# Layer 1's grouped product computed once in quarter-width tiles, with layer 0's full-array scores in place of its row-tiled transposed scores

## The chip, the core and the metric

The kernel runs on one NeuronCore of a Trainium2 chip. It has five engines that run side by side: TensorE (PE, matrix products; its weight loads are listed as PEld), VectorE (DVE), ScalarE (ACT), GpSimd (POOL) and SyncE (SP, which here only starts DMA transfers). Products land in PSUM, a small memory of eight banks of 128 partitions by 512 f32 values; DVE and ACT read it, POOL and DMA don't. SBUF is the working memory.

The metric is the device time of one execution in microseconds. Three runs of the kernel before took 5622.65, 5635.56 and 5646.51 us: the median is 5635.56.

## The reference

The input x is 2 images of 128 channels, 256 by 256, in f32. Two blocks follow each other, each a residual block: normalise (groups of 4 channels, over each image), apply the layer, add the input.

Layer 0 is windowed attention with a halo:

```python
qkv = einsum('bchw,oc->bohw', x, W_qkv)            # 128 -> 3*128, 4 heads of 32
q = 8x8 windows of q                               # 64 queries a window
k, v = 12x12 windows of k, v, step 8, padded by 2  # 144 keys a window
attn = (q * SCALE) @ k.T + rel_pos_emb(q) + FIXED_MASK
out = softmax(attn) @ v                            # back to the image
return einsum('bchw,oc->bohw', out, W_out)
```

The fixed mask is minus infinity except where row and column distance between query and key have the right parity. So the 64 queries of a window fall into four classes of 16 (row parity, column parity), and each class sees 36 of the 144 keys. The relative position term adds, for each query, one value by the column distance and one by the row distance.

Layer 1 is:

```python
t1 = conv(x, w1)                    # 5x1, 128 -> 128 channels
t3 = conv(t1, w3)                   # 3x1, each channel by itself
t2 = three copies of x, shifted by -2, 0, 2 columns
t4 = einsum('nckhw,ckg->nghw', t2, w4)   # 3*128 -> 8 channels
return t4[:, None] * t3.reshape(n, 16, 8, h, w)   # the 8 channels repeat 16 times
```

So t4 has 8 channels, and channel c of the output uses channel c mod 8 of t4.

## The kernel before

`kernel_body` runs three stages in a row: `attention_fast` (layer 0, lines 122 to 391), `in_range` (a test of the softmax denominators) and `convolutions_fast` (layer 1). After them a branch runs a second, complete implementation, `tile_halo_attention_then_conv`, if a denominator left its range; on the inputs at hand the branch isn't taken. Names of tiles in `attention_fast` begin with f_, and layer 1's tiles are xm, w, t, a, b, y, raw.

The image is worked in strips of 8 rows: 32 strips an image, 64 in all. In between, layer 0's output x1 lies in DRAM.

**Layer 0** begins with the statistics of image 0 (f_sx loads, line 88), about 92 us. Then it works units of one row parity of a strip: 128 units, two for each strip. The normalised strip is stored by row and column parity, so that all operands of a class lie together. A unit u does:

- `scores` (line 281): for each of 4 heads and 2 column parities ("lanes", 8) a 60 by 512 block of transposed scores, 60 keys of a pair of windows on partitions, 512 queries as columns. A lane uses 32 rows (one head's channels) and 60 columns of the array. It is filled by accumulation of 8 products for the column term (f_rw), 4 for the row term (f_rh) and 16 for the keys, one for each pair of windows (f_kt): 28 products in each of 8 lanes, 224 a unit.
- `numerators` (line 302): exponentials, with the mask as bias, no maximum subtracted.
- `values` (line 258): 32 products of 128 rows by 60 columns, copied from PSUM to f_vt by DVE (6 of 8 copies) and ACT (line 263).
- `attend` (line 317): 128 products of 60 rows by 32 columns, 33 moving columns (32 channels and the denominator), followed by reciprocal, scaling and a 32 by 32 block transpose on DVE (`head_outputs`).
- `project` (line 342), `queries` (line 245) and `keys` (line 232): products of the full array with 512 columns.

The order of PE's instructions in layer 0 is written out by hand (`manual_schedule`); the other engines' order, and layer 1's, is set by the scheduler.

**Layer 1** works strip by strip. For each strip k: normalise 8 rows (line 442, DVE; POOL copies 4 rows of overlap, line 440); t1 by four groups of five products, 128 by 128 weights and 512 columns, one for each tap of w1 (line 482), copied by ACT (486); t3 by one ACT scaling (488) and two DVE multiply-adds over 2048 values (490); then for each two rows t4 by three products (line 497), of which the weights w4 are tiled 16 times so that all 128 output channels come out, and y = t4 times t3 by DVE from PSUM (501); two additions of the input by POOL (505, 506) and a store from POOL's queue (507). So t4 costs 12 products of 512 columns a strip. PSUM: three banks for a, three for b.

Of the kernel before, what the change touches and what calls it, by code (L numbers as in the profile page):

```python
# [10 lines left out]
I32 = mybir.dt.int32  # L11
# [5 lines left out]
PE = mybir.EngineType.PE  # L17
# [9 lines left out]
XC = 130  # L27
XW = 272

DEN_LOW, DEN_HIGH = 1.0e-24, 1.0e36  # L30

# [9 lines left out]
def host_constants():  # L46
    ident = np.eye(P, dtype=np.float32)
    gavg = np.zeros((P, P), np.float32)
    for g in range(P // 4):
        gavg[4 * g : 4 * g + 4, 4 * g : 4 * g + 4] = 0.25  # L50

    kb = np.zeros((HEADS, 32, 6, 10), np.float32)
    for c in range(10):
        kb[:, c, :, c] = 1.0
    for r in range(6):
        kb[:, 10 + r, r, :] = 1.0
    kb[:, 16, :, 6:] = NEG
    kb[:, 17, :, :4] = NEG
    flag = np.zeros((2, 4 * NPAIR * 4, 2, 4), np.float32)
    flag[0, :, 0] = 1.0  # L60
    flag[1, :, 1] = 1.0

    mask = np.full((2, 64, 2), NEG, np.float32)
    for key in range(60):
        c = key // 6
        mask[:, key, 0] = 0.0 if c < 6 else NEG
        mask[:, key, 1] = 0.0 if c >= 4 else NEG
    return {
        "c_ident": ident,
        "c_gavg": gavg,  # L70
        "c_kb": kb.reshape(P, 60),
        "c_flag": flag.reshape(2, 4 * NPAIR, 32),
        "c_mask": mask.reshape(P, 2),
    }


class Norms:


    def __init__(self, nc, glob, small, gavg, ns):  # L80
        self.nc, self.glob, self.small, self.gavg, self.ns = nc, glob, small, gavg, ns

    def new(self, name, tag):
        return self.glob.tile([P, self.ns * 4, 6], F32, tag=tag, name=name)

    def chunk(self, st, n, t):
        for c in range(t.shape[1] // 2):
            self.nc.vector.bn_stats(  # L88
                st[:, n + c, :], t[:, 2 * c : 2 * c + 2, :].rearrange("p a w -> p (a w)")
            )  # L90

    def group(self, st, ps_pool, name):
        nc, glob, small, gavg = self.nc, self.glob, self.small, self.gavg
        mv = small.tile([P, 2], F32, tag="mv", name=f"mv_{name}")
        nc.vector.bn_aggr(mv, st.rearrange("p n k -> p (n k)"))  # L95
        pm = ps_pool.tile([P, 512], F32, tag="pj", name=f"pm_{name}")
        nc.tensor.matmul(pm[:, 0:1], gavg, mv[:, 0:1], start=True, stop=True)
        mean = glob.tile([P, 1], F32, tag=f"mean_{name}", name=f"mean_{name}")
        nc.vector.tensor_copy(mean, pm[:, 0:1])
        d = small.tile([P, 1], F32, tag="d", name=f"d_{name}")  # L100
        nc.vector.tensor_sub(d, mv[:, 0:1], mean)
        q = small.tile([P, 1], F32, tag="q", name=f"q_{name}")
        nc.vector.tensor_mul(q, d, d)
        nc.vector.tensor_add(q, q, mv[:, 1:2])
        pv = ps_pool.tile([P, 512], F32, tag="pj", name=f"pv_{name}")
        nc.tensor.matmul(pv[:, 0:1], gavg, q, start=True, stop=True)
        v = small.tile([P, 1], F32, tag="v", name=f"v_{name}")
        nc.vector.tensor_scalar(v, pv[:, 0:1], 1e-5, None, ALU.add)
        sd = small.tile([P, 1], F32, tag="sd", name=f"sd_{name}")
        nc.scalar.activation(sd, v, AF.Sqrt)  # L110

        r0 = small.tile([P, 1], F32, tag="r0", name=f"r0_{name}")
        nc.vector.reciprocal(r0, sd)
        nc.vector.tensor_mul(r0, r0, v)
        nc.vector.tensor_add(r0, r0, sd)
        nc.vector.tensor_scalar(r0, r0, 0.5, None, ALU.mult)
        rstd = glob.tile([P, 1], F32, tag=f"rstd_{name}", name=f"rstd_{name}")
        nc.vector.reciprocal(rstd, r0)
        return mean, rstd


def attention_fast(tc, io, x1_d, norm, st_x, st_y, tags, rc_all):

    nc = tc.nc
    x = io["x"]
    NB, _, H, _ = x.shape
    NS = H // 8
    NU = 2 * NB * NS
    with ExitStack() as l0:
        cst = l0.enter_context(tc.tile_pool(name="f_cst", bufs=1))  # L130
        ps_pj = l0.enter_context(tc.tile_pool(name="f_pj", bufs=2, space=PSUM))
        ps_s = l0.enter_context(tc.tile_pool(name="f_s", bufs=1, space=PSUM))
        ps_o = l0.enter_context(tc.tile_pool(name="f_o", bufs=1, space=PSUM))

        def cload(name, src, shape):
            t = cst.tile(shape, F32, tag=f"f_{name}", name=f"f_{name}")
            nc.sync.dma_start(t, src)
            return t

        wqkvT = cload("wqkvT", io["w_qkvT"], [P, 3 * P])  # L140
        woT = cload("woT", io["w_outT"], [P, P])
        mask = cload("mask", io["c_mask"], [P, 2])
        rw = cload("rw", io["rw"], [P, 8, 60])
        rh = cload("rh", io["rh"], [P, 4, 60])
        wq_s = cst.tile([P, P], F32, tag="f_wq_s", name="f_wq_s")
        nc.scalar.mul(wq_s, wqkvT[:, 0:P], SCALE)
        wkT = wqkvT[:, P : 2 * P]
        wvT = wqkvT[:, 2 * P : 3 * P]

        xn = [cst.tile([P, 2, 2, XC, 6], F32, tag=f"f_xn{i}", name=f"f_xn{i}") for i in range(2)]  # L150
        kt = [
            [cst.tile([P, 2, XC, 6], F32, tag=f"f_kt{r}{i}", name=f"f_kt{r}{i}") for i in range(2)]
            for r in range(2)
        ]
        vt = [
            cst.tile([P, NPAIR, HEADS, 33], F32, tag=f"f_vt{i}", name=f"f_vt{i}") for i in range(2)
        ]
        sc = [ps_s.tile([P, 512], F32, tag=f"s{h}", name=f"f_s{h}") for h in range(HEADS)]
        for i in range(2):
            nc.gpsimd.memset(xn[i], 0.0)  # L160
            for r in range(2):
                nc.gpsimd.memset(kt[r][i], 0.0)
            nc.gpsimd.memset(vt[i], 1.0)
        for h in range(HEADS):
            nc.vector.memset(sc[h], 0.0)

        with ExitStack() as setup:
            sp = setup.enter_context(tc.tile_pool(name="f_setup", bufs=6))
            for s in range(NS):
                t = sp.tile([P, 8, W], F32, tag="sx", name=f"f_sx_0_{s}")  # L170
                nc.sync.dma_start(t, x[0, :, 8 * s : 8 * s + 8, :])
                norm.chunk(st_x[0], 4 * s, t)

        rawp = l0.enter_context(tc.tile_pool(name="f_raw", bufs=4))
        x1p = l0.enter_context(tc.tile_pool(name="f_x1", bufs=2))
        wk = l0.enter_context(tc.tile_pool(name="f_wk", bufs=2))

        raws, norms, qs, pts, ots, x1s, po = {}, {}, {}, {}, {}, {}, {}

        def stats_chunk(b, c):  # L180

            t = rawp.tile([P, 4, W], F32, tag="sx", name=f"f_sx_{b}_{c}", bufs=2)
            nc.sync.dma_start(t, x[b, :, 4 * c : 4 * c + 4, :])
            norm.chunk(st_x[b], 2 * c, t)

        def load_rows(k):

            b, s = divmod(k, NS)
            t = rawp.tile([P, 10, W], F32, tag="raw", name=f"f_raw_{k}")
            n = min(10, H - 8 * s)  # L190
            nc.sync.dma_start(t[:, 0:n, :], x[b, :, 8 * s : 8 * s + n, :])
            raws[k] = t

        def normalise(k):
            b, s = divmod(k, NS)
            if s == 0:
                norms[b] = norm.group(st_x[b], ps_pj, f"x{b}")
                st_y[b] = norm.new(f"st_y{b}", tags[(2 * b + 2) % 3])
                if b + 1 < NB:
                    st_x[b + 1] = norm.new(f"st_x{b + 1}", tags[(2 * b + 1) % 3])  # L200
            mean, rstd = norms[b]
            cur, prev = xn[k % 2], xn[(k + 1) % 2]
            cells = cur.rearrange("p r c j i -> p (r c) j i")
            if s == 0:
                nc.gpsimd.memset(cells[:, :, :, 0:1], 0.0)
                lo = 0
            else:
                nc.gpsimd.tensor_copy(
                    cells[:, :, :, 0:2], prev.rearrange("p r c j i -> p (r c) j i")[:, :, :, 4:6]
                )  # L210
                lo = 1
            hi = min(10, H - 8 * s) // 2
            rows = raws[k].rearrange("p (i r) (j c) -> p c r j i", r=2, c=2)
            for c in range(2):
                nc.vector.tensor_scalar(
# [119 lines left out]
        def project(u, half):  # L335
# [14 lines left out]
            if half == 1:  # L350
                nc.gpsimd.dma_start(x1_d[b][s][:, r:8:2, :], x1)  # L351
                norm.chunk(st_y[b], 4 * s + 2 * r, x1)
                if r == 1:
                    del raws[k]
# [183 lines left out]
def in_range(tc, glob, rc_all):  # L538
# [19 lines left out]
    return good  # L558

# [555 lines left out]
```

## Time and profile before

| | us |
|---|---|
| median of three runs | 5635.56 |
| the profiled execution's own time | 5622.65 |
| its span, first to last instruction | 5620.7 |
| start: statistics of image 0 | 0 to 97.6 |
| layer 0 | 97.6 to 3829.3 |
| range test, statistics of layer 0's output | 3829.3 to 3844.7 |
| layer 1 | 3844.7 to 5620.7 |

| line, engine | what | count | mean ns |
|---|---|---|---|
| L486 ACT | a to t, 128 by 512 | 254 | 585 |
| L488 ACT | t3 scaling, 128 by 2048 | 64 | 2002 |
| L490 DVE | multiply-add, 128 by 2048 | 128 | 2530 |
| L442 DVE | normalise, 128 by 2048 | 62 | 1338 |
| L263 DVE | f_pv to f_vt, 60 by 512 | 768 | 687 |
| L332 DVE | transpose, 128 by 512 | 256 | 711 |

How the page is read: busy time is the time in which an engine worked on something, and the idle time behind a bar "|" is that of the engine just before an instruction of the group, with what ended it. "issue" is idle time that nothing in the profile explains. The granted clock is the share of TensorE's full clock. The chain goes back from the last instruction, at each step to what released it.

### The profile page before, as it was taken

To read this page: it belongs to the slowest core of one execution; us is meant where nothing else is said; L and a number is where in the kernel's file an instruction comes from. 1 tells how busy PE (TensorE), PEld (TensorE's weight loads), DVE (VectorE), ACT (ScalarE), POOL (GpSimd) and SP (SyncE) were. 2 spreads that over 40 slices of the span, in tenths; PEclk is the share of its full clock that TensorE was granted. 3 is DMA by queue.
4 is the path that set the end of the run, shared out by engine and by line. 5 is a ranking of instruction groups with operands and counts; after the bars stand their busy time and mean duration, and the time that the engine had idled before them with its cause. 6 is when DMAs were issued, how large, how long until landed. Compare 5 with 4: busy or idle time off the path is not lost.

```text
span 5620.7 us, 217714 instructions
## 1 busy us (share of the span) xinstructions
PE 4597.4 (82%) x103982; PEld 2896.5 (52%) x103982; DVE 2227.0 (40%) x3705; ACT 1131.0 (20%) x2133; POOL 844.7 (15%) x656
## 2 busy tenths in 40 slices
PE   2677777777777777777777777778999999999998
PEld 1555555555555555555555555554444444444443
DVE  8754334343433444334343433434333333333333
ACT  1122222222222222222222222221111111111111
POOL 1000000000000000000000000002322232333222
PEclk9778878787778788778878887888999999999999
DMA  8521111111111111111111111102222222222221
GB/s 323 196 79 50 37 41 50 41 50 41 48 43 35 50 41 50 41 37 50 41 50 41 50 41 37 48 22 79 79 79 75 75 75 75 75 81 76 82 75 50
DMA packets 71310, 367.08 MB, mean 65 GB/s; under 512 B 8080, under 2 KB 8848, under 8 KB 49936
## 3 DMA queue, kind: packets, MB, share of 16 engines
q1 hardware_dynamic: 42768, 218.82, 11.8%
q0 software_dynamic: 27648, 134.23, 5.9%
q8 instruction: 818, 13.40, 1.0%
q14 instruction: 76, 0.62, 0.0%
HBM read 218.80 MB, written 134.22 MB: 63 GB/s over the span
## 4 chain that ended last, share of the span: by engine, by line
PE 76%; issue 15%; DVE 6%; DMA 2%; ACT 1%; SPq 0%; POOL 0%; ACTq 0%; POOLq 0%; DVEq 0%
PE a L482 19%; PE f_s L281 17%; PE b L497 12%; PE f_pv L258 10%; PE f_o L317 6%; DVE f_vt L263 5%; PE f_pk L232 4%; PE f_pq L245 4%; PE f_py L342 3%; DMA f_sx<-in_x 2%; ACT f_vt L263 1%; DVE f_st_x L88 1%; DVE st_x L88 0%; PE a_first L468 0%; DVE mv_x L95 0%
## 5 line engine op out<-in xcount | busy, mean ns | idle before, releaser
L263 DVE COPY f_vt<-f_pv 60x512 f32<-60x512 f32 x768 | 527.4, 687 | 1751.4 <-PE f_pv L258 1742.5
L482 PE MATMUL a<-xm,w 128*128 128x512 f32 (+1 forms) x2560 | 1105.6, 589 | 0.0
L281 PE MATMUL f_s<-f_q,f_kt 32*60 32x32 f32 x32768 | 522.8, 264 | 375.7 <-issue 375.7
L258 PE MATMUL f_pv<-f_wqkvT,f_xn 128*60 128x128 f32 x8192 | 758.2, 356 | 71.3 <-DVE f_vt L263 56.0
L482 PEld LDWEIGHTS a<-xm,w 128*128 128x128 f32 x2560 | 480.9, 188 | 614.5 <-issue 613.3
L302 ACT ACTIVATE f_p<-f_s,f_mask 128x256 f32<-128x256 f32 x1024 | 388.0, 488 | 1795.8 <-PE f_s L281 1795.8
L258 PEld LDWEIGHTS f_pv<-f_wqkvT,f_xn 128*60 128x60 f32 x8192 | 665.1, 181 | 141.6 <-PE f_pv L258 82.1
L490 DVE SCALAR_TENSOR_TENSOR t<-t,w,t 128x2048 f32<-128x2048 f32 x128 | 323.8, 2530 | 1014.1 <-ACT t L486 1011.9
L281 PEld LDWEIGHTS f_s<-f_q,f_kt 32*60 32x60 f32 x32768 | 498.2, 175 | 409.0 <-issue 408.1
L497 PE MATMUL b<-xm,w 128*128 128x512 f32 x1536 | 669.5, 591 | 0.0
L351 POOL DMA_DIRECT2D f_x<-f_x x128 | 91.2, 713 | 2955.8 <-DVE f_x L345 2955.8
L281 PE MATMUL f_s<-f_q,f_rw 32*60 32x64 f32 x16384 | 258.1, 252 | 295.5 <-issue 295.5
L497 PEld LDWEIGHTS b<-xm,w 128*128 128x128 f32 x1536 | 289.5, 189 | 368.9 <-issue 367.2
L486 ACT COPY t<-a 128x512 f32<-128x512 f32 (+1 forms) x256 | 149.3, 583 | 1451.9 <-PE a L482 1451.9
L317 PEld LDWEIGHTS f_o<-f_vt,f_p 60*32 60x32 f32 x32768 | 303.2, 105 | 224.8 <-issue 125.2
L281 PEld LDWEIGHTS f_s<-f_q,f_rw 32*60 32x60 f32 x16384 | 219.7, 145 | 317.5 <-issue 312.2
L281 PE MATMUL f_s<-f_q,f_rh 32*60 32x128 f32 x8192 | 314.4, 406 | 71.2 <-issue 71.2
L317 PE MATMUL f_o<-f_vt,f_p 60*32 60x33 f32 x32768 | 334.4, 201 | 28.3 <-issue 26.6
L342 PE MATMUL f_py<-f_ot,f_woT 128*128 128x512 f32 x512 | 287.3, 649 | 45.0 <-ACT f_vt L263 32.6
L281 PEld LDWEIGHTS f_s<-f_q,f_rh 32*60 32x60 f32 x8192 | 231.9, 175 | 101.9 <-issue 100.5
L232 PE MATMUL f_pk<-f_xn,f_wqkvT 128*128 128x512 f32 (+1 forms) x528 | 266.5, 625 | 4.3 <-issue 3.0
L506 POOL TENSOR_TENSOR y<-y,raw 128x1280 f32<-128x1280 f32 x64 | 244.7, 3823 | 127.4 <-DVE y L501 127.4
(90 smaller groups left out, 3043.9 us busy)
## 6 DMA issues: line engine op xcount, KB each, us to landing
f_raw<-in_x SPq DMA_DIRECT2D x62, 1280.0 KB, 6.8
f_x<-f_x POOLq DMA_DIRECT2D x128, 512.0 KB, 5.2
out<-y POOLq DMA_DIRECT2D x64, 1024.0 KB, 4.2
raw<-f_x SPq DMA_DIRECT2D x64, 640.0 KB, 4.2
f_sx<-in_x SPq DMA_DIRECT2D x32, 1024.0 KB, 12.2
f_sx<-in_x SPq DMA_DIRECT2D x64, 512.0 KB, 3.6
raw<-f_x SPq DMA_DIRECT2D x62, 384.0 KB, 4.8
f_raw<-in_x SPq DMA_DIRECT2D x2, 1024.0 KB, 5.6
```

What stands on the lines that cost most here:

```text
L232: nc.tensor.matmul(pk[:, : n * P], wkT, xt[:, r, c, 1:129, lo:hi], start=True, stop=True)
L245: nc.tensor.matmul(pq, wq_s, xn[k % 2][:, r, c, 1:129, 1:5], start=True, stop=True)
L258: nc.tensor.matmul(pv[64 * c : 64 * c + 60, P * n : P * n + P], xt[:, r, c, col : col + 10].rearrange("p j i -> p (j i)"), wvT, start=True ...
L263: (nc.scalar.copy if c and j > 1 else nc.vector.tensor_copy)(vt[u % 2][64 * c : 64 * c + 60, 4 * j : 4 * j + 4, :, 0:32], pv[64 * c : 64 * ...
L281: nc.tensor.matmul(out, w, m, start=start, stop=stop, skip_group_check=True)
L302: nc.scalar.activation(p[:, h].rearrange("p (n e q) -> p n e q", e=2, q=16)[:, :, e], sc[h].rearrange("p (n e q) -> p n e q", e=2, q=16)[: ...
L317: nc.tensor.matmul(po[c][32 * h : 32 * h + 32, n, :], p[rows, h, 32 * m : 32 * m + 32], v[rows, m, h, :], start=True, stop=True,)
L342: nc.tensor.matmul(py, woT, ots.pop((u, half)), start=True, stop=True)
L482: nc.tensor.matmul(pa[:, : n * W], w1[:, tap, :], xt[:, j - 2 + tap : j - 2 + tap + n, 2 : 2 + W], start=tap == 0, stop=tap == 4,)
L490: nc.vector.scalar_tensor_tensor(t3, t1[:, tap : tap + 8, :], w3[:, tap : tap + 1], t3, ALU.mult, ALU.add)
L497: nc.tensor.matmul(pb, w4[:, tap, :], xt[:, j + 1 : j + 3, 2 * tap : 2 * tap + W], start=tap == 0, stop=tap == 2,)
L506: nc.gpsimd.tensor_tensor(y[:, 3:8, :], y[:, 3:8, :], raws[b, s][:, 0:5, :], ALU.add)
```

## The change

Two things change together.

Layer 0 is now the first half of `tile_halo_attention_then_conv`, which the program before held behind the branch; `attention_fast`, `in_range`, `convolutions_fast` and the branch go. Its work:

- A strip is worked in 8 units i: four classes ab (row and column parity), each in two halves of 8 pairs of windows. 512 units in all.
- `queries` (once a class): one product of 512 columns, copied by four ACT copies of 32 partitions into a block-diagonal tile qbd (two buffers).
- `unfold` (once a class): POOL copies the normalised strip to xu, 60 keys of each of 16 pairs of windows together.
- `biases` (once a strip): 32 products, 128 by 128 weights wb and 64 columns; 16 ACT copies of 16 partitions put the terms into abd (one buffer), 16 rows of bias terms and two mask flags for each head.
- `scores`: for each of 8 pairs of windows two products with 128 weight columns (4 heads by 32 queries) and 60 moving columns (keys): qbd with the keys, and abd with the constant kb. So scores lie with queries on partitions. DVE takes the maximum and subtracts it, ACT exponentiates.
- `transposes`: four 128 by 128 transposes on TensorE, copied by DVE or ACT in turn, before `attend`, which has the products of before.
- No order is written out by hand.

Layer 1 computes t4 once, for 8 channels padded to 32: four row pairs j go to four 32-partition blocks of one PSUM bank, 12 products with 32 weight columns. ACT copies the bank to t4; then for each j one product with a 0/1 matrix (32 rows, 128 columns) spreads the 8 channels to 128. In the program's order one product of the next strip's t1 stands ahead of these four. PSUM: two banks for a, one for g, four for b.

```diff
-        ps_a = l1.enter_context(tc.tile_pool(name="ps_a", bufs=3, space=PSUM))
-        ps_b = l1.enter_context(tc.tile_pool(name="ps_b", bufs=3, space=PSUM))
+        ps_a = l1.enter_context(tc.tile_pool(name="ps_a", bufs=2, space=PSUM))
+        ps_g = l1.enter_context(tc.tile_pool(name="ps_g", bufs=1, space=PSUM))
+        ps_b = l1.enter_context(tc.tile_pool(name="ps_b", bufs=1, space=PSUM))
...
-        w4 = cst.tile([P, 3, P], F32, tag="w4", name="w4")
+        w4 = cst.tile([P, 3, 32], F32, tag="w4", name="w4")
+        sel = cst.tile([P, P], F32, tag="sel", name="sel")
+        nc.sync.dma_start(sel, io["c_sel"])
...
+            pg = ps_g.tile([P, 512], F32, tag="g", name=f"g_{k}")
+            for tap in range(3):
+                for j in range(4):
+                    nc.tensor.matmul(
+                        pg[32 * j : 32 * j + 32, :], w4[:, tap, :],
+                        xt[:, 2 * j + 1 : 2 * j + 3, 2 * tap : 2 * tap + W],
+                        start=tap == 0, stop=tap == 2,
+                    )
+            t4 = wk.tile([P, 512], F32, tag="t4", name=f"t4_{k}")
+            nc.scalar.copy(t4, pg)
...
-            for j in range(0, 8, 2):
-                pb = ps_b.tile([P, 512], F32, tag="b", name=f"b_{k}_{j}")
-                for tap in range(3):
-                    nc.tensor.matmul(
-                        pb, w4[:, tap, :], xt[:, j + 1 : j + 3, 2 * tap : 2 * tap + W],
-                        start=tap == 0, stop=tap == 2,
-                    )
+            for j in range(4):
+                pb = ps_b.tile([P, 512], F32, tag=f"b{j}", name=f"b_{k}_{j}")
+                nc.tensor.matmul(
+                    pb, sel[32 * j : 32 * j + 32, :], t4[32 * j : 32 * j + 32, :], start=True, stop=True
+                )
...
-        kernel_body(tc, io, out)
+        tile_halo_attention_then_conv(tc, io, out)
```

The functions of layer 0 that take over, from the kernel after:

```python
def biases(k):
    xv = xn[k % 2].rearrange("p r (k c) -> p r c k", c=16)
    for t1 in range(4):
        pa = ps_pj.tile([P, 512], F32, tag="pj", name=f"pa_{k}_{t1}")
        for v in range(8):
            ...
            nc.tensor.matmul(
                pa[:, 64 * v : 64 * v + 64],
                wb[:, t1, v].rearrange("p h r -> p (h r)"),
                xv[:, 2 + 2 * t1 : 4 + 2 * t1, c : c + 2, k0 : k0 + NPAIR],
                start=True, stop=True,
            )
        for h in range(HEADS):
            nc.scalar.copy(
                abd[32 * h : 32 * h + 16, :, :, h, t1, :].rearrange("p k n v -> p (k n) v"),
                pa[32 * h : 32 * h + 16, :].rearrange("p (v m) -> p m v", v=8),
            )

def scores(i):
    k, g = divmod(i, 8)
    ab, half = divmod(g, 2)
    ps = ps_s.tile([P, 8, 64], F32, tag="s", name=f"s_{i}")
    for j in range(8):
        c0 = 8 * (8 * half + j)
        dst = ps[:, j, 0:60]
        nc.tensor.matmul(
            dst, qbd[ab % 2][:, 8 * half + j].rearrange("p h t v -> p (h t v)"),
            kt[k % 2][:, ab, :, c0 : c0 + 10], start=True, stop=False,
        )
        nc.tensor.matmul(
            dst, abd[:, ab, 8 * half + j].rearrange("p h t v -> p (h t v)"), kb,
            start=False, stop=True,
        )
    mx = wk.tile([P, 8, 1], F32, tag="mx", name=f"mx_{i}")
    nc.vector.tensor_reduce(mx, ps[:, :, 0:60], AX.X, ALU.max)
    p = pt[i % 3]
    nc.vector.tensor_tensor(p[:, :, 0:60], ps[:, :, 0:60], mx.to_broadcast([P, 8, 60]), ALU.subtract)
    nc.scalar.activation(p[:, :, 0:60], p[:, :, 0:60], AF.Exp)

def transposes(i):
    p = pt[i % 3]
    pp = ps_t.tile([P, 4, P], F32, tag="t", name=f"t_{i}")
    for j in range(4):
        nc.tensor.transpose(pp[:, j, :], p[:, 2 * j : 2 * j + 2, :].rearrange("p a b -> p (a b)"), ident)
    t = wk.tile([P, 4, P], F32, tag="ptT", name=f"ptT_{i}")
    if i % 2:
        nc.scalar.copy(t, pp)
    else:
        nc.vector.tensor_copy(t, pp)
    pts[i] = t
```

The other functions of layer 0 (`queries`, `keys`, `unfold`, `values`, `attend`, `head_outputs`, `project`) do per class or half what the description above says.

## The prediction

> **What bounds the kernel now.** I read the page's busy shares and slices first, then the busy time by stage, then the groups, then the order of time inside a stage.
>
> ```profile
> PE 4597.4 (82%) x103982; PEld 2896.5 (52%) x103982; DVE 2227.0 (40%) x3705; ACT 1131.0 (20%) x2133; POOL 844.7 (15%) x656
> ...
> PE   2677777777777777777777777778999999999998
> ...
> PEclk9778878787778788778878887888999999999999
> ...
> PE 76%; issue 15%; DVE 6%; DMA 2%; ACT 1%; SPq 0%; POOL 0%; ACTq 0%; POOLq 0%; DVEq 0%
> PE a L482 19%; PE f_s L281 17%; PE b L497 12%; PE f_pv L258 10%; PE f_o L317 6%; DVE f_vt L263 5%; PE f_pk L232 4%; PE f_pq L245 4%; PE f_py L342 3%; DMA f_sx<-in_x 2%; ACT f_vt L263 1%; DVE f_st_x L88 1%; DVE st_x L88 0%; PE a_first L468 0%; DVE mv_x L95 0%
> ```
>
> TensorE sets the time: 76% of the chain that ended last is its work, with 15% of "issue". The slices show two stages. Windows cut at their ends (us; busy time and count of PE, PEld, DVE, ACT, POOL; clock, DMA share, GB/s):
>
> ```profile
> 97.60:3829.30 3731.70, 2835.14 (x99860) 2119.90 (x99860) 1551.68 (x3085) 849.45 (x1805) 292.46 (x318) 0.80 0.16 52
> 3844.70:5620.70 1776.00, 1758.57 (x4108) 773.46 (x4108) 576.43 (x449) 278.02 (x322) 531.23 (x322) 0.99 0.20 74
> ```
>
> Layer 0 takes 3731.7 us, 58.3 us for each of 64 strips, at a mean clock of 0.80 with PE 76% busy. Layer 1 takes 1776.0, 27.75 a strip, PE 99% busy: what leaves PE there shortens the kernel, down to the next limit (DVE 9.0 us a strip, POOL 8.3).
>
> ```profile
> L482 PE MATMUL a<-xm,w 128*128 128x512 f32 x2540 | 1101.3, 590 | 0.0
> L482 PEld LDWEIGHTS a<-xm,w 128*128 128x128 f32 x2560 | 480.9, 188 | 614.5 <-issue 613.3 <-POOL y L505 0.5
> L281 PE MATMUL f_s<-f_q,f_kt 32*60 32x32 f32 x32768 | 522.8, 264 | 375.7 <-issue 375.7
> L235 ACT COPY f_kt<-f_pk 128x512 f32<-128x512 f32 x256 | 155.0, 606 | 95.6 <-PE f_pk L232 95.6
> L501 DVE TENSOR_TENSOR y<-b,t 128x512 f32<-128x512 f32 x256 | 170.7, 688 | 161.6 <-PE b L497 155.0 <-DVE t L490 1.1
> ```
>
> Line 482 issues 1280 products and the trace holds 2560 loads: an f32 product is two pairs of weight load and matmul. The timeline gives the price of a pair by its shape:
>
> ```profile
> 1923.16 0.30 PEld L97 LDWEIGHTS pm_x<-mv_x,f_gavg 128*128 128x128 f32 x2
> ...
> 3016.43 0.87 PEld L258 LDWEIGHTS f_pv<-f_wqkvT,f_xn 128*60 128x60 f32 x16 [0.76 <-PE f_pv L258]
> 3016.46 1.09 PE L258 MATMUL f_pv<-f_wqkvT,f_xn 128*60 128x128 f32 x16 [0.54 <-DVE f_vt L263]
> ...
> 3021.47 1.29 PE L317 MATMUL f_o<-f_vt,f_p 60*32 60x33 f32 x128
> 3022.69 1.99 PE L245 MATMUL f_pq<-f_xn,f_wq_s 128*128 128x512 f32 x4
> ...
> 4507.09 17.34 PE L482 MATMUL a<-xm,w 128*128 128x512 f32 x40
> ```
>
> - 512 columns: 0.43 us a pair (17.34/40), the load hidden behind the stream.
> - 128 weight columns, one moving column: two loads take 0.30 us and one 0.19, so the second costs 0.11. A product with few columns is bound by its load.
> - Values (L258), two column tiles side by side: 1.09 us for 16 pairs.
> - Heads (L317), eight tiles: (3022.69 - 3021.47)/128 = 0.0095 us a pair.
>
> **The change, part by part.** *Layer 0* gets full-array scores. Out, per strip: 448 row-tiled products (896 pairs). The chain puts f_s at 17% (956 us), and the waits put 742 us on "issue" in front of f_s: 26.5 us a strip together. Also out are the waits of the values for DVE's copies (f_vt, 5%, 4.4 us a strip): the new order has other groups between two value groups, and ACT takes half of the copies. In or kept, on PE per strip (8 units of 16 windows, in the order of the built program):
>
> - scores: 128 products, 256 pairs x 0.11 = 28.2 us (60 moving columns stream in 0.43 x 60/512 = 0.05, so the load binds);
> - position biases: 32 products, 64 pairs x 0.11 = 7.0;
> - transposes: 32. Every f32 product of the trace is two pairs: 64 x 0.11 = 7.0. Lower end one pair, 3.5;
> - kept work: values 8 x 1.09 = 8.7; heads 512 x 0.0095 = 4.9; queries, keys and projection 12 products, 24 x 0.43 = 10.3;
> - change of shape between groups, 24 a strip: f_pq starts 0.07 before the modelled end of f_o, so little is lost; 0.1 each, 2.4 (ends 0 and 6.7, the 0.28 by which f_pq's 1.99 exceeds 4 x 0.43).
>
> 68.5 us. Not shown before: queries and keys now stream every second column (before, runs of four), and the biases' columns lie 64 bytes apart. Bounds: nothing, or the stream of 8 products at half rate, 8 x 0.86 = 6.9 us; below nothing it can't go, since f_pq streams as fast as the contiguous L482. I take nothing, by f_pq; the biases are bound by their loads.
>
> Waits: `abd` has one buffer, so a new strip's bias copies follow the old strip's last scores. From there: first bias group 1.8, 16 ACT copies x 0.606 = 9.7, one exponential 0.6, four query copies 2.4 = 14.5 us before the next scores; PE has 11.3 to do (7.0 + heads 0.6 + transposes 0.9 + queries 0.9 + values 1.1 + projection 0.9): 3.2 idle. The three later query blocks each wait for four copies and an exponential (0.9 + 0.1 + 2.4 + 0.6 = 4.0 against 3.4 of PE work): 0.6 x 3 = 1.8. Behind the waiting scores stand the next values and heads. Sum 73.5 us a strip; ends 64 (transposes of one pair, no idle at the start, free changes of shape) and 80 (dear changes of shape, query waits doubled). DVE: per unit a maximum and a subtraction over 480 (0.65 each by L501's rate), copies, head outputs, about 4.4 us of 9.2; ACT 4.2; POOL's unfolding (960 elements four times a strip, 1.1 to 2.0 ns each by its strided copies L208 and L227) 4 to 8 of 73, on two buffers: all beside PE. SP's row loads shrink from ten rows to eight; the DMA engines were 16% busy. 64 x 73.5 = 4704, against 3731.7: **+972**.
>
> [...]
>
> [...]
>
> *Head and seam.* The range test goes (two reductions of 4.4 us at 3824 to 3834, -9); 64 small bias-weight copies on DVE come into the start (0.16 each by the one-column rows, +10), where DVE is busy with statistics. Nothing net; new POOL memsets lie beside the 92 us of loads.
>
> *Layer 1.* Out: 24 pairs x 0.43 = 10.3 us a strip. In: 24 pairs in four 32-column tiles, and 8 pairs in four 32-row tiles. Two column tiles ran fully side by side in f_pv (0.87/16 = 0.054 a pair against 0.43 x 128/512 = 0.107), eight tiles of f_o at least 2.9-fold (0.43 x 33/512 = 0.0277 against 0.0095). I take fourfold: 2.6 + 0.9, plus four changes of shape at 0.15: 4.1, saving 6.2. Twofold (5.2 + 1.7 + 0.6) saves 2.8; not at all (13.7 + 0.6) costs 4.0. The new wait (product, ACT copy 0.6, spread) is covered by the next strip's first product, 0.86, which stands ahead of the spread; if ACT were late, the other 19 products queue behind it. The normalisation of the next strip now stands behind the first tap: 0.6 + 2.0 + 2.5 + 1.3 after the sixth row, 6.8 with hand-overs against 4.3 + 2.6 on PE: just covered. The small weights' and the selector's loads lie ahead of the stage. 64 x 6.2 = **-397**.
>
> Sum: the profiled run's 5622.65 (span 5620.7 and 2 around it) + 972 - 397 = 6198. That run was the fastest of three, 13 below the median: **6210 us**.
>
> **Rivals.**
> 1. *Faster: the score loads overlap each other.* 320 pairs a strip; each 0.01 us is 205 us, so under 0.08 a pair the kernel is faster than before. At the streaming limit of 0.05 it takes 6210 - 1230 = 4980. For it: eight-tile loads overlap in L317. Against: L97's pairs stream a single column and still come 0.11 apart.
> 2. *Layer 0 loses less:* transposes of one pair (-224) and no idle at strip starts (-205): 5780. For: DVE and ACT under half busy; against: the single `abd`.
> 3. *The clock.* Before, layer 0 ran at 0.80 on the mean: after gaps on "issue" the clock fell to 0.5 for several us. The new stream has a third fewer instructions and shorter gaps, so I take full clock. At 0.80 its 68.5 us become 86: +1100, 7300.
> 4. *Layer 1's tiles do not run side by side:* +4.0 in place of -6.2 a strip, 6860; at twofold, 6430.
>
> **How the numbers follow.** My forecast (6000 to 6450) 0.50; rival 2 (5600 to 6000) 0.20, of which 0.03 within 0.5%; rival 3 0.10; rival 4 0.10; rival 1 0.10. About 0.5% (28 us) is what a measurement of this kernel can tell from no change. Faster 0.10, same 0.03, slower 0.87. The range, 5720 to 6900, leaves out rival 1 and the tail of rival 3; it holds rival 2's sum and rival 4's, and strided streams at half rate (6650).
>
> **What would show it.** Layer 0 near 4700 us with score loads 0.11 apart; t products twice or once per transpose; PE idle about 3 us before the first scores of a strip, ended by ACT; clock near 1; layer 1 near 1380 with four g matmuls starting within 0.1 us. Score pairs under 0.08, or a clock of 0.8, make it wrong.

## The result and the profile after

The kernel after takes 6175.03 us (median of four runs, 6154.85 to 6200.46) against 5641.03 for the kernel before (four runs): 1.0954 times as long, 95% interval 1.0902 to 1.1007. The forecast was 6210 us. The profiled execution took 6200.46 us; the prediction's sum for it was 6198 (the profiled execution of before plus the two terms). By the medians the change costs 534 us, where the forecast had 574 (6210 against 5635.56).

The same stages as before, cut at their ends (us; busy time and count of PE, PEld, DVE, ACT, POOL; granted clock, DMA share, GB/s):

```profile
103.80:4799.00 4695.20, 4524.11 (x65042) 3797.67 (x65042) 2113.41 (x4037) 2033.22 (x3597) 534.00 (x766) 0.94 0.11 37
4816.00:6198.70 1382.70, 1366.59 (x4617) 536.23 (x4616) 601.29 (x448) 315.50 (x386) 470.19 (x322) 0.99 0.26 96
```

Layer 0 went from 3731.7 to 4695.2 us (+963.5; forecast +972), layer 1 from 1776.0 to 1382.7 (-393.3; forecast -397). The start before layer 0 grew by 6.2 us and the seam between the layers by 1.6. The four add up to 578.0, the whole difference of the two spans.

On the page, PE is now almost always busy, and the clock is nearly full, where before it lay at 7 to 8 tenths throughout layer 0:

```profile
PE 5899.2 (95%) x69684; PEld 4339.8 (70%) x69684; DVE 2814.9 (45%) x4720; ACT 2353.2 (38%) x3993; POOL 1039.0 (17%) x1112
...
PE   3999999999999999999999999999999999999998
...
PEclk9999899998999999899999999999999999999999
```

The groups of instructions on PE (line, out<-in, shape, count; busy us, mean ns of one; idle before, and what ended it):

```profile
L322 PE MATMUL s<-kt,qbd 128*128 128x60 f32 x8192 | 1687.5, 289 | 12.4 <-ACT qbd L294 4.1
L326 PE MATMUL s<-kb,abd 128*128 128x60 f32 x8192 | 1677.2, 289 | 0.0
...
L305 PE MATMUL pv<-wqkvT,xu 128*60 128x128 f32 x8192 | 631.0, 293 | 59.6 <-DVE x L402 57.4 <-ACT abd L282 1.2 <-issue 1.0
...
L342 PE MATMUL t<-ident,pt 128*128 128x128 f32 x2048 | 337.9, 289 | 19.0 <-ACT pt L334 18.9
...
L396 PE MATMUL py<-ot,woT 128*128 128x512 f32 x512 | 280.2, 629 | 78.6 <-ACT abd L282 76.8 <-DVE ot L382 1.8
...
L551 PE MATMUL g<-xm,w 128*32 128x512 f32 x1536 | 178.8, 598 | 0.0
L568 PE MATMUL b<-t,sel 32*128 32x512 f32 x512 | 73.0, 640 | 0.7 <-ACT t L557 0.7
```

Three things are to be seen. The score products (L322, L326) are 256 records a strip, as counted. The transposes (L342) are 2048 records in 64 strips, 32 a strip: one pair of load and matmul for each transpose, not two. And there is no "issue" in front of the scores any more; the 742 us of it before are gone.

The waits of PE over the whole run (releaser: us in total, times, longest):

```profile
PE py L396 <- ACT abd L282: 76.8, 63, 1.2
PE pv L305 <- DVE x L402: 57.4, 61, 0.9
PE t L342 <- ACT pt L334: 18.9, 103, 0.5
...
PE s L322 <- ACT qbd L294: 4.1, 4, 1.3
```

The first two come once in a strip, at its start. The timeline of one strip's start (start us, length, engine, line, group, count; in brackets the idle time before):

```profile
2548.77 5.58 PE L275 MATMUL pa<-xn,wb 128*128 128x64 f32 x48
...
2558.62 1.09 PE L305 MATMUL pv<-wqkvT,xu 128*60 128x128 f32 x16
2560.93 1.12 PE L396 MATMUL py<-ot,woT 128*128 128x512 f32 x2 [1.23 <-ACT abd L282]
2563.00 0.40 PE L305 MATMUL pv<-wqkvT,xu 128*60 128x128 f32 x2 [0.94 <-DVE x L402]
2563.33 0.43 PE L322 MATMUL s<-kt,qbd 128*128 128x60 f32 x2
2563.60 0.54 PE L326 MATMUL s<-kb,abd 128*128 128x60 f32 x2
2563.93 0.64 PE L322 MATMUL s<-kt,qbd 128*128 128x60 f32 x2
2564.36 0.63 PE L326 MATMUL s<-kb,abd 128*128 128x60 f32 x2
```

After 1.23 and 0.94 us of idle within 3 us, the rows of the scores, of two pairs each, no longer start 0.22 us apart, as they do elsewhere, but 0.43: the granted clock has halved, from 1.0 to 0.5. The clock's records show 39 such stretches, 612.8 us in all. 36 of them begin 14 to 15 us after the first bias product (L275) of a strip, behind these two waits, and all but one of these last 10.2 or 20.5 us. But only some strips have one: of 63, 27 have no such stretch, though nearly all have the two waits. Those 27 take 69.2 us, the others mostly 73.7 or 78.3; the mean is 73.4.

Layer 1, the grouped product of one strip and its spread:

```profile
5006.67 0.16 PEld L551 LDWEIGHTS g<-xm,w 128*32 128x32 f32 x8 [0.76 <-issue]
5006.67 2.79 PE L551 MATMUL g<-xm,w 128*32 128x512 f32 x24
...
5007.13 0.13 PEld L551 LDWEIGHTS g<-xm,w 128*32 128x32 f32 x4 [0.30 <-issue]
...
5009.39 1.13 PE L542 MATMUL a<-xm,w 128*128 128x512 f32 x2
...
5009.55 0.58 ACT L557 COPY t<-g 128x512 f32<-128x512 f32 x1 [2.19 <-PE g L551]
...
5010.45 1.14 PE L568 MATMUL b<-t,sel 32*128 32x512 f32 x8
```

The loads of g come in fours, and the 24 pairs take 2.72 us until line 542 goes on: 0.113 us a pair against 0.43 for the full array. The copy by ACT ends at 5010.13, the product of the next strip at 5010.52: the new wait is covered.

### The profile page after: what moved, and what is told of

Same layout as the page of the kernel before. It is cut to its first block, busy times and chain, and to the rows that moved or that the text cites. A ratio compares the mean times of both kernels' runs of the same rounds, so it can differ in the third digit from the quotient of the medians.

```text
span 6198.7 us, 152584 instructions
## 1 busy us (share of the span) xinstructions
PE 5899.2 (95%) x69684; PEld 4339.8 (70%) x69684; DVE 2814.9 (45%) x4720; ACT 2353.2 (38%) x3993; POOL 1039.0 (17%) x1112
## 5 line engine op out<-in xcount | busy, mean ns | idle before, releaser
L322 PE MATMUL s<-kt,qbd 128*128 128x60 f32 x8192 | 1687.5, 289 | 12.4 <-ACT qbd L294 4.1
L326 PE MATMUL s<-kb,abd 128*128 128x60 f32 x8192 | 1677.2, 289 | 0.0
L322 PEld LDWEIGHTS s<-kt,qbd 128*128 128x128 f32 x8192 | 1352.2, 206 | 111.9 <-ACT qbd L294 95.0
L326 PEld LDWEIGHTS s<-kb,abd 128*128 128x128 f32 x8192 | 1350.6, 207 | 0.0
L294 ACT COPY qbd<-pq 32x512 f32<-32x512 f32 x1024 | 590.1, 576 | 718.3 <-PE pq L290 707.0
L305 PEld LDWEIGHTS pv<-wqkvT,xu 128*60 128x60 f32 x8192 | 485.0, 141 | 393.5 <-issue 272.0
L282 ACT COPY abd<-pa 16x512 f32<-16x512 f32 x1024 | 590.0, 576 | 392.4 <-PE pa L275 378.6
L305 PE MATMUL pv<-wqkvT,xu 128*60 128x128 f32 x8192 | 631.0, 293 | 59.6 <-DVE x L402 57.4
L275 PE MATMUL pa<-xn,wb 128*128 128x64 f32 x4096 | 487.0, 291 | 0.0
L275 PEld LDWEIGHTS pa<-xn,wb 128*128 128x128 f32 x4096 | 467.5, 192 | 3.2 <-ACT kt L257 0.3
## 6 DMA issues: line engine op xcount, KB each, us to landing
sx<-in_x SPq DMA_DIRECT2D x32, 1024.0 KB, 10.3
```

The costliest lines, as they stand in the source:

```text
L275: nc.tensor.matmul(pa[:, 64 * v : 64 * v + 64], wb[:, t1, v].rearrange("p h r -> p (h r)"), xv[:, 2 + 2 * t1 : 4 + 2 * t1, c : c + 2, k0 : ...
L282: nc.scalar.copy(abd[32 * h : 32 * h + 16, :, :, h, t1, :].rearrange("p k n v -> p (k n) v"), pa[32 * h : 32 * h + 16, :].rearrange("p (v ...
L294: nc.scalar.copy(qbd[ab % 2][32 * h : 32 * h + 32, :, h].rearrange("p n t v -> p t n v"), pq[32 * h : 32 * h + 32, :].rearrange("p (t n v) ...
L305: nc.tensor.matmul(pv[r0 : r0 + 60, P * (j // 2) : P * (j // 2) + P], xu[ab % 2][:, 8 * half + j].rearrange("p r c -> p (r c)"), wvT, star ...
L322: nc.tensor.matmul(dst, qbd[ab % 2][:, 8 * half + j].rearrange("p h t v -> p (h t v)"), kt[k % 2][:, ab, :, c0 : c0 + 10], start=True, sto ...
L326: nc.tensor.matmul(dst, abd[:, ab, 8 * half + j].rearrange("p h t v -> p (h t v)"), kb, start=False, stop=True,)
```

## The experiments

The main theory to be tested: layer 0 is a sum of weight loads (a score pair costs its load), layer 1 gains by four tiles side by side, and the two parts don't disturb each other. The rivals: the parts interact; the half clock at strip starts has another cause than the idle time there; the pair's price is not the load. A ratio below is always to the kernel before, run on the same chip; kernels that ran on different chips are compared by these ratios.

### Each part alone

e1 has layer 0 of before and layer 1 of after. e2 has layer 0 of after and layer 1 of before.

In e1, against the kernel before:

```diff
-            for j in range(0, 8, 2):
-                pb = ps_b.tile([P, 512], F32, tag="b", name=f"b_{k}_{j}")
-                for tap in range(3):
-                    nc.tensor.matmul(
-                        pb, w4[:, tap, :], xt[:, j + 1 : j + 3, 2 * tap : 2 * tap + W],
...
+            pg = ps_g.tile([P, 512], F32, tag="g", name=f"g_{k}")
+            for tap in range(3):
+                for j in range(4):
+                    nc.tensor.matmul(
+                        pg[32 * j : 32 * j + 32, :], w4[:, tap, :],
...
```

In e2, against the kernel after, the same lines the other way round:

```diff
-            pg = ps_g.tile([P, 512], F32, tag="g", name=f"g_{k}")
...
+            for j in range(0, 8, 2):
+                pb = ps_b.tile([P, 512], F32, tag="b", name=f"b_{k}_{j}")
...
```

> The kernel before with layer 1 of the kernel after (quarter-width tiles and the spread), layer 0 as before. Theory (the two parts add: layer 1 saves about 397 us by itself, because TensorE was busy 99% of its 1776 us): 5641 - 395 = about 5245 us, layer 1 near 1380 us, layer 0 still near 3730 us. Rival (the saving comes only together with the other layer 0, or the next limit of layer 1 is met): layer 1 above 1500 us, the whole above 5400 us.

> The kernel after with layer 1 as it was before (12 products of 512 columns with 128 weight columns a strip). Theory (the parts add): 6175 + 395 = about 6570 us, layer 0 near 4695 us as in the kernel after, layer 1 near 1776 us; against the kernel before +930 us, all of it layer 0's. Rival: under 6400 us, which would say that part of what layer 1 saves was not its own.

Measured: e1 5271.81 us, ratio 0.9316 (0.9304 to 0.9329), 387 us less than before. e2 6562.9 us, ratio 1.1618 (1.1585 to 1.1650), 904 us more. The two differences from 1 add to +0.093, the change's own is +0.095 (its interval 0.090 to 0.101): the parts add, and neither gives the other anything. The part in layer 1 is worth having without the other: e1 is faster than both kernels.

### The idle time at a strip's start, and the clock

In e3 the bias copies, all on ACT in the kernel after, go to DVE for every second group.

```diff
-                    nc.scalar.copy(
+                    (nc.vector.tensor_copy if t1 % 2 else nc.scalar.copy)(
                         abd[32 * h : 32 * h + 16, :, :, h, t1, :].rearrange("p k n v -> p (k n) v"),
```

> The kernel after, with two of the four bias groups of each strip copied by DVE and the other two by ACT. The wait at a strip's start (about 2.2 us of TensorE idle, in front of a projection and a value group) rests on 16 ACT copies in a row; it should go. Theory A (the idle costs what it lasts): -140 us, about 6035, clock in layer 0 still 0.94. Theory B (the idle is also what lowers the clock: 37 of the 39 stretches at half clock begin some 12 to 15 us after a strip's start): the half-clock stretches go too, 4.2 us a strip: 6175 - 140 - 270 = about 5765 us, clock 0.98 or more. Theory C (DVE's own queue takes over the wait): within 40 us of 6175.

Measured: 5813.71 us, ratio 1.0275 (1.0260 to 1.0291), so 361 us less than the kernel after, 383 by the ratios; of the three theories the second (5765) is nearest. Layer 0 by windows, and the largest waits of PE that are left in its strips:

```profile
103.80:4425.00 4321.20, 4263.10 (x64978) 3571.57 (x64978) 2463.41 (x4549) 1750.01 (x3084) 534.05 (x766) 0.99 0.12 40
```

```profile
PE t L342 <- ACT pt L334: 37.8, 113, 0.5
PE s L322 <- ACT qbd L294: 8.2, 16, 0.8
```

Both waits at the strip's start are gone, 134 us, and with them nearly all half-clock time: 90.5 us in 6 stretches in place of 612.8 in 39, which by itself is worth up to 522/2 = 261 us. So idle time of some 2.2 us in a strip cost more through the clock (up to 261 us) than as idle time (134). The stretches went with these waits: TensorE's products are the same in both kernels. (The scheduler, though, also moved 50 head products in front of the waiting projection in most strips, so idle time and order changed together.)

Idle time is not all of it, since 27 strips of the kernel after have none of the stretches. The clock's records show more. In the traces of before and after all changes of the clock (390 and 78) lie on one grid of 3.413 us, to within 0.004 us. For each step of this grid at full clock, add up the columns that its products stream, each weighted by the share of the 128 by 128 array that it fills; at 512 in 0.43 us some 4060 fill a step. In the kernel after, away from both ends of the run, 32 of the 38 steps just before a fall of the clock lie below 1400, and none of the 1560 others; in the kernel before 193 of 193 and 48 of 971. The same count gives 213 of 237 and 40 of 958 in e4, below. It separates less well in e9 (117 of 119, but 191 of 1098). So in these four runs the clock mostly fell behind steps in which little of the array streamed, and idle time lowers this sum too. That this sum is the cause was not shown: no run set it on purpose.

### What a score pair costs

e4 halves the moving columns of the score products: the scores of the first 30 keys of each block stand in for all 60, so the scores of the other 30 keys are left out. e5 is e3 with half of the weight columns: two of the four heads get no scores (the expectation counts heads up to 7; the kernel has four).

e4, against the kernel after:

```diff
-                dst = ps[:, j, 0:60]
+                dst = ps[:, j, 0:30]
...
-                    kt[k % 2][:, ab, :, c0 : c0 + 10], start=True, stop=False,
+                    kt[k % 2][:, ab, 0:3, c0 : c0 + 10], start=True, stop=False,
...
```

e5, against e3:

```diff
-                dst = ps[:, j, 0:60]
+                dst = ps[0:64, j, 0:60]
...
-                    dst, qbd[ab % 2][:, 8 * half + j].rearrange("p h t v -> p (h t v)"),
+                    dst, qbd[ab % 2][:, 8 * half + j, 0:2].rearrange("p h t v -> p (h t v)"),
...
-                    dst, abd[:, ab, 8 * half + j].rearrange("p h t v -> p (h t v)"), kb,
+                    dst, abd[:, ab, 8 * half + j, 0:2].rearrange("p h t v -> p (h t v)"), kb,
```

> The kernel after, each score product streaming 30 of its 60 moving columns (half of the keys are left out; the other half of the columns is a copy, so that the softmax has its size). Theory (a pair is bound by its weight load of 128 columns): score loads still 0.112 us apart, the time within 40 us of 6175. Rival 1 (the stream binds): pairs 0.06 apart, 6175 - 256 x 0.055 x 64 = about 5275 us. Rival 2 (the clock follows the columns that stream): more half-clock time, 6300 us or more.

> The kernel of e3 (5813.71 us, clock 0.992), and in the score and bias products 64 weight columns in place of 128: query head pairs 0 and 1 only, so that heads 4 to 7 get no scores, and the weights' rows for them are left at their first filling. Moving columns stay 60. Theory A (a score pair costs its weight load, which goes with the weight columns): pair 0.112 to between 0.053 (what 60 moving columns cost by the fourfold layer 1 products: 2.72 us / 24 pairs x 4 / 512 x 60) and 0.058; 256 x 0.054 = 13.8 us a strip less, x64 = 885: about 4930 us at full clock. Theory B (a pair costs something fixed, the same for any size, such as the issue of its instructions): pair stays at 0.112 and the time at 5814. With the clock rule of e4 the clock stays near 1, because the share of time with columns streaming grows.

Measured: e4 7107.88 us, ratio 1.2535 (1.2483 to 1.2588), 14% more than the kernel after by the ratios, with half of the streaming. e5 5055.26 us, ratio 0.8937 (0.8922 to 0.8952), 758 us less than e3.

Two pairs of a score product at full clock, first in e4, then in e5:

```profile
2506.10 0.39 PE L322 MATMUL s<-kt,qbd 128*128 128x30 f32 x2
2506.32 0.39 PE L326 MATMUL s<-kb,abd 128*128 128x30 f32 x2
2506.54 0.39 PE L322 MATMUL s<-kt,qbd 128*128 128x30 f32 x2
```

```profile
2507.74 0.20 PEld L322 LDWEIGHTS s<-kt,qbd 128*64 128x64 f32 x2
2507.86 0.20 PEld L326 LDWEIGHTS s<-kb,abd 128*64 128x64 f32 x2
2507.98 0.20 PEld L322 LDWEIGHTS s<-kt,qbd 128*64 128x64 f32 x2
```

In e4, score loads at full clock still come 112 ns apart, as in the kernel after: a pair costs the same with 30 moving columns as with 60. In e5 they come 58 ns apart (median of 15698 gaps; 98% of them lie between 55 and 59), within the 0.053 to 0.058 that was expected of half the weight columns. So a score pair of the kernel after costs its load, and half of the weight columns make it cheaper, 0.058 us for 0.112. Whether the 58 ns of e5 are still the load, 56 by half of 112, or already the stream of 60 columns, 50 to 53, these runs don't tell. Of the 13.8 us a strip that were expected, 12.6 came in the score groups (29.6 to 17.0 in strips at full clock); the last load of each score group now waits longer for what follows (203 ns in the median, 112 in e3).

The loss in e4 is the clock. Its page, and the only wait of a strip's start that it has left:

```profile
PE 6933.6 (97%) x69684; PEld 5180.9 (73%) x69684; DVE 2708.7 (38%) x5232; ACT 2364.6 (33%) x3993; POOL 1038.0 (15%) x1112
...
PEclk8777777777777777777677777777677799999999
```

```profile
PE pv L305 <- DVE x L405: 56.4, 60, 0.9
```

PE counts as 97% busy and waits no longer than in the kernel after, yet the clock's mean falls from 0.951 to 0.795, with 2927.7 us at half clock. What was halved is the time in which columns stream: per pair 30 columns, 0.43 x 30/512 = 0.025 us, in 0.112 us of loading, against 0.050 in the kernel after. So between these two kernels the clock went with the share of time with columns streaming, by this estimate 0.22 in e4 and 0.45 in the kernel after, not with the share that the profile calls busy, 97% and 95% (rival 3 of the prediction, by another road). In e5, where a pair streams for 0.050 of 0.058 us, the clock is 0.996, as good as in e3 (0.992). Weighted by the share of the array, the score products of e5, which fill half of it, come to 0.43.

In the kernel after the clock halved behind 2.2 us of idle in two pieces, and in e4 mostly behind none: 201 of the 237 grid steps before a fall hold no idle time of PE.

### What a transpose costs

e7 is e3 with each transpose of the probabilities written as an ordinary product by the identity.

```diff
-                nc.tensor.transpose(pp[:, j, :], p[:, 2 * j : 2 * j + 2, :].rearrange("p a b -> p (a b)"), ident)
+                nc.tensor.matmul(
+                    pp[:, j, :], p[:, 2 * j : 2 * j + 2, :].rearrange("p a b -> p (a b)"), ident,
+                    start=True, stop=True,
+                )
```

> The kernel of e3 (5813.71 us), and each of the 32 transposes of the probabilities in a strip written as an ordinary product by the identity matrix. Theory A (an f32 transpose goes through TensorE once, an f32 product twice): the 32 go from 3.75 us to 32 x 2 x 0.112 = 7.2 us a strip, +3.4 x 64 = +220: about 6035 us. Theory B (a transpose was already the same work, and the count of records only hides it): 5814.

Measured: 6016.47 us, ratio 1.0640 (1.0623 to 1.0658), 203 us more than e3. The group of transposes:

```profile
L342 PE MATMUL t<-ident,pt 128*128 128x128 f32 x4096 | 605.9, 288 | 13.2 <-ACT pt L334 13.1
```

4096 pairs in place of 2048, and 3.2 us a strip more: each of these f32 transposes is one pair of load and matmul, written as an f32 product it is two. The second theory would have had no change.

### What makes the four column tiles run side by side

e6 is the kernel after with the two loops of g exchanged, so that the three taps of one tile follow each other.

```diff
-            for tap in range(3):
-                for j in range(4):
+            for j in range(4):
+                for tap in range(3):
```

> The kernel after, and in layer 1 the 12 quarter-width products of a block are issued with the three taps of one column tile after each other, in place of one tap through the four column tiles. Same products, same result. Theory A (the side-by-side running needs neighbours in the queue that lie in different column tiles): three products in a row in the same tile follow each other, only every fourth neighbour overlaps; the group goes from 2.72 us to between 6 and 10.3 us for 24 pairs, x64 blocks, +210 to +490 us: 6390 to 6660. Theory B (each column tile has its own queue, which runs ahead of the others): 2.7 us, and the time stays at 6175.

Measured: 6341.31 us, ratio 1.1248 (1.1185 to 1.1312), 166 us more than the kernel after; just outside the lower end of the first theory, 5.4 us for the group where it had 6 to 10.3. One strip's g on the timeline:

```profile
5008.08 5.43 PE L551 MATMUL g<-xm,w 128*32 128x512 f32 x24
5013.44 1.13 PE L542 MATMUL a<-xm,w 128*128 128x512 f32 x2
```

Twofold, neither fourfold (2.72 us) nor one after another (24 x 0.43 = 10.3). The scheduler kept the order of the source: in the built program the twelve products stand tile by tile. An estimate in which products start strictly in the order of the program, and a tile overlaps only the last pair of the tile before it, gives 6 + 5 + 5 + 5 = 21 steps of 0.43, 9.0 us. It took twelve. By the start times of the 24 matmuls, one starts in each of the first two steps, two in the next two, three in the four after them, and so down again. So more of them ran side by side than in that estimate, and fewer than in the kernel after. What decides how many was not shown; what was measured is that the order of the two loops makes 2.72 or 5.43 us of the same products.

### Layer 0 of before, with the new layer 1

Since the two parts add, the better kernel has layer 0 of before. e8 is e1 with the value products of the next unit put between the score groups, and the queries ahead of the first heads. e9 is e8 with the bursts of short products parted by long ones.

e8, against e1:

```diff
+            if u + 1 < NU:
+                values(u + 1, (0,))
             for t in range(4):
                 for h, c in lanes:
...
+                if u + 1 < NU and n in (5, 11):
+                    values(u + 1, (2 if n == 5 else 3,))
...
-                if u + 1 < NU:
-                    values(u + 1)
...
+                if u + 1 < NU:
+                    queries(u + 1)
                 if u < NU:
                     attend(u, 0)
...
```

e9, against e8:

```diff
-                    attend(u, 0)
+                    attend(u, 0, 0)
+                    if nxt:
+                        queries(u + 1, (1,))
+                    attend(u, 0, 1)
                     head_outputs(u, 0)
...
-                    attend(u, 1)
+                    attend(u, 1, 0)
+                    if nxt:
+                        keys(u + 1, (1,))
+                    attend(u, 1, 1)
```

> The kernel of e1 (layer 0 of before, layer 1 of after; 5271.81 us, clock 0.846), and in each of the 128 units of layer 0 the four value groups of the next unit are issued between the score products of this one, and the next unit's queries ahead of this unit's first heads. Same work. Theory A (in before's layer 0 TensorE loses about 3 us a unit to waits between stages, and the clock falls with each): up to 3 x 128 = 384 us less, and a clock nearer 1: 4600 to 4900. Theory B (the value groups were what hid the exponentials, and moved away they leave that wait open): 0 to +250 us: 5270 to 5520.

> The kernel of e8 (5043.03 us, clock 0.892), and in each unit of layer 0 the bursts of short products are parted by long ones: each half's 128 products o in two pieces of 64 with a query or key product between them, a value group between the last of them and the next unit's scores, another ahead of the first. Same work. In e8 TensorE still stands still for 700 us with nothing to wait for in the profile (f_s 369.1, f_o 306.3), most of it in the middle of such bursts. Theory A (bursts outrun a supply of instructions, which catches up while long products stream): these stops fall under 350 us, and the clock rises; 350 to 600 us less: 4450 to 4700 us. Theory B (the supply is short over the whole unit, or the stops have another cause): the stops move elsewhere and stay near 700 us in sum; 5000 to 5090 us.

Measured: e8 5043.03 us, ratio 0.8919 (0.8901 to 0.8937); e9 5044.85 us, ratio 0.8896 (0.8881 to 0.8910). By the ratios e8 takes 4.3% less than e1, about 225 us, and e9 as long as e8, the intervals overlapping.

e8 fell between its two theories. The waits for the copies of the values are gone (53.1 and 33.5 us in e1, 2.0 and 4.0 in e8), and the exponentials stayed covered (PE waits 2.1 us for them in front of f_o). But most of the time on "issue" stayed, first e1, then e8:

```profile
PE f_s L285 <- issue: 750.0, 444, 4.3
...
PE f_o L321 <- issue: 45.1, 17, 4.6
```

```profile
PE f_s L285 <- issue: 369.1, 270, 2.8
...
PE f_o L327 <- issue: 306.3, 154, 5.8
```

e9's second theory held for the time, but only in part for the stops: in front of f_o there are 104 us less, in front of f_s 22 more, 593.6 us of the two in sum against 675.4.

```profile
PE f_s L286 <- issue: 391.1, 375, 2.4
PE f_o L326 <- issue: 202.5, 126, 4.7
```

Half-clock time fell too, from 1087 to 745 us, and still the kernel is no faster. So these stops and the clock don't account for the time of e9 by themselves; where the gain went isn't shown. The timeline of e9 shows such stops in the middle of bursts wherever the bursts lie:

```profile
2011.63 0.76 PE L326 MATMUL f_o<-f_vt,f_p 60*32 60x33 f32 x64
2012.43 1.13 PE L250 MATMUL f_pq<-f_xn,f_wq_s 128*128 128x512 f32 x2
2013.49 0.57 PE L326 MATMUL f_o<-f_vt,f_p 60*32 60x33 f32 x42
2015.84 0.32 PE L326 MATMUL f_o<-f_vt,f_p 60*32 60x33 f32 x22 [1.78 <-issue]
```

A cause that fits, but that no run here tests by itself: the supply of instructions. The page of before lists 818 transfers of the kind "instruction" on queue q8, 13.40 MB, so 16 KB each. 783 of them start in its layer 0, one for 255 PE instructions (a load and a matmul count as two), and they hardly ever start less than 3.3 us apart (0.4% of the gaps lie below 3.3, 47% of them between 3.3 and 3.8). If these are PE's instructions, which the trace doesn't say, that makes 13 ns an instruction (3.3 us / 255, an estimate). A pair of the heads takes 0.0095 us, so under 5 ns an instruction. In layer 0 of after, where pairs are long, these transfers are 9.2 us apart in the mean, and there is no "issue" in front of its scores. What would settle it, the same products with fewer instructions, wasn't tried.

## Why the prediction was right

The total and both stages came out within 1% of the forecast. Partly this is luck. The sum was made for the profiled execution of before, the fastest of its kernel, and is compared with that of after, the slowest of its four; by the medians the two parts alone are +904 (e2) and -387 us (e1), against +972 and -397. And inside layer 0 three terms were off and cancelled. The table sets the prediction's steps, per strip, beside a strip of the kernel after at full clock (411.5 to 480.6 us of the trace), with PE's time from one weight load to the next given to the line of the first, and the idle time taken out. The half clock is the difference of the mean strip, 73.4, to a clean one, 69.2.

| step | predicted us | measured us |
|---|---|---|
| scores, 256 pairs | 28.2 | 29.1 |
| biases, 64 pairs | 7.0 | 7.5 |
| transposes, 32 | 7.0 | 3.75 |
| values | 8.7 | 8.6 |
| heads | 4.9 | 5.6 |
| queries, keys, projection, with the changes of shape | 12.7 | 11.9 |
| idle | 5.0 | 2.6 |
| half clock | 0 | 4.2 |
| sum | 73.5 | 73.3 |

- *Scores by their load, 0.11 a pair.* Right: 0.112, with 30 moving columns (e4) as with 60, and 0.058 with half of the weight columns (e5). Taken from a row of single-column loads before, it held for 60 columns. Rival 1 (loads overlap, a pair under 0.08) is out.
- *Transposes as two pairs.* Wrong; this is the term that was mis-sized. "Every f32 product of the trace is two pairs" was carried over to a transpose, of which TensorE had none in the trace of before. It is one pair, -3.3 us a strip, 208 in all (e7: 203). The lower end of the step held the truth.
- *Waits.* The place was right, and for 1.2 us the releaser (ACT's copies into abd); another 0.9 us ended with DVE's addition to a projection. The size was not: 2.2 us in place of 3.2. PE waits there in front of the projection and the values, not the scores. The waits of the later query blocks, 1.8, are next to nothing (4.1 us in the whole run).
- *Clock taken as full.* Wrong in size: 0.94 in layer 0, 4.2 us a strip, 270 in all. The prediction had a lower clock as rival 3, but at the 0.80 of the kernel before, and had not joined it to its own idle time of 3.2 us. In e3 the two went together, so that its step "no idle at the strip's start", put at 205 us in rival 2, is worth 361 to 383.
- *Strided streams of queries and keys, taken as free.* Nearly right: the matmuls of keys and queries start 0.46 us apart at full clock, those of line 542 0.43, so 16 pairs cost some 0.4 us a strip more, far from the 6.9 of half rate.
- *Changes of shape.* 2.4 us together with the 12 large products gave 12.7, against 11.9 measured. Over all PE steps but the transposes, the strip takes 3.6 us more than the bare prices of its pairs; for 24 changes that is 0.15 each at most, not the 0.28 of the step's upper end.
- *Layer 1 fourfold.* Right: 2.72 us for g and 1.07 for the spread, 3.8 against 4.1 with changes of shape; -393 against -397. Rival 4 is out, but e6 shows that it hung on the order: with the loops exchanged the same products run twofold, 5.43 us.
- *Nothing net for head and seam.* +7.8 us.

Rival 2 lay at 5780: with transposes of one pair, as is the case, and without the idle time, e3 took 5813.71. Its two conditions were half true in the kernel after, and the clock took back what the first had given.

## What to carry to other kernels

Price a product with few moving columns by its weight load (here 0.112 us a pair with 128 weight columns, for 30 moving columns as for 60), and count the pairs: here two for an f32 product, one for an f32 transpose (4096 and 2048 records for the same tiles). Where PE idles once in a period of 70 us, even for 2 us, look for slower products behind it, and add the clock to the price of the wait (in the kernel after 134 us of waits, and 612.8 us at half clock). The same goes for products that keep PE busy and stream little (0.795 in e4). When a change has two parts, price them apart: here one alone was worth -387 us and the other alone cost 904, and the good one could be kept alone (0.93 of the time before), and with a reordered layer 0 (0.89).

## What had not been expected of the hardware

- In 36 of 63 strips the clock stays at half, mostly for 10.2 or 20.5 us, after some 2.2 us of idle time, and a kernel whose PE is 97% busy lay at 0.795 with 30 columns streaming for each load in place of 60 (e4): halving the moving columns of a product made the kernel 14% slower.
- The 24 pairs of four column tiles took 2.72 us with neighbours in the program in different tiles, fourfold speed, and 5.43 us, twofold, with six pairs of a tile behind each other.
- Bursts of products of 0.01 us a pair stop for 1 to 2 us in the mean with nothing to wait for in the profile, some 600 to 800 us in layer 0 of before, e1, e8 and e9, in each of the orders that were run.
